# Layer 0's masks through PSUM, fewer small instructions for lists and norms, and a re-ordered layer 3 in a four-layer graph-attention kernel

## The chip, the cores and the metric

The kernel runs on one core of a Trainium2 chip. The core has five instruction queues: PE (the matrix engine; PEld is its weight load, which runs beside the matmuls), DVE (VectorE), ACT (ScalarE), POOL (GpSimd) and SP (SyncE, which here only issues DMAs). Each queue works in order. PE reads from SBUF and writes to PSUM, which has 8 banks of 128 x 512 fp32. The metric is the device time of one execution in microseconds (us), less is better. The kernel before takes 2305.02 us, the median of 3 runs (2301.89 to 2305.65).

## What is computed

There are 4096 nodes with 256 features, and an adjacency matrix of 0.4% ones plus the diagonal. Four layers of graph attention follow each other, each as `x = layernorm(x + gnn(x, adj))`. Layers 0 and 1 have four heads of 64 columns, layer 2 has two heads of 128. Cut to what matters, a head is

```
h   = x @ W                                    # values
e   = leaky_relu(s1[i] + s2[j], 0.2)           # s1, s2: h times two vectors
att = softmax over j of (e where adj[i, j], else -inf)
out = att @ h
```

Layer 3 has one score, but two softmaxes of it, one over `e` and one over `-e`; the second is subtracted, the two results go through one matrix product and an ELU.

## The kernel before

**Tiles and lists.** Rows (destinations) are worked in 32 tiles of 128. Few nodes have an edge into a given tile, so for each tile the kernel makes a list of those that do, in 13 groups of 128, and the compact mask that belongs to it. A 14th group, at place FRONT = 6, is the tile's own 128 nodes, which need no list. So a tile has 14 places, worked in two halves of 7. The lists are made once, while layer 0 runs (`lists`): ACT turns the int32 adjacency into bytes (L373), DVE finds which nodes occur (L377), and per tile `pack` builds 31 one-hot matrices on DVE (L430), with which PE compacts the mask (L436). Each mask row carries four more columns, three of which are the node's number in base 16, so that the matmul compacts the numbers too. ACT copies the 128 mask columns (L443) and, apart, the digit columns (L444) out of PSUM; DVE makes indices of the digits (L448 to L451). The mask goes to DRAM as `maskC`. Ten tiles are packed before layer 0 begins; the other 22 one by one in its first 22 tiles.

**A tile in a layer.** `RowTile.load` issues the DMAs of a half: on SP the score row `S` (L620) and the compact mask `mk` (L622), the tile's own nodes directly (L627), the residual (L926); on POOL one indirect DMA per listed group (L630), 13 per tile, 1456 in all, which gather value rows and scores of 128 nodes into a slot `G`. The slots are a ring; in layer 0 there are 16 of two groups each, some 2.3 tiles. `RowTile.half` computes the weights. exp(leaky_relu) is written as a maximum of an exponential and a constant: for three heads in layers 0 and 1 (both in layer 2) ACT does the exponential for each group (L671), and DVE in one instruction of 896 columns the maximum with LEAST and the product with the mask (L672). The fourth head in layers 0 and 1 needs no exponential: DVE multiplies each group's scores and takes the maximum (L667, seven per half), then multiplies by the mask (L668). In layer 1, and only there, DVE first copies a whole tile's mask bytes as int32 into a PSUM bank (L646), and L668 and L672 read them there; in the other layers they read `mk` in SBUF. Layer 3 has its own form (L658 to L662). PE multiplies weights and values (L680, L683). `finish` divides, adds the residual and calls `norm`, which works out 1/sqrt with 15 small DVE instructions (L945 to L955) for a group of rows' tiles and then scales them (L957); in layer 0 groups are of four up to tile 24, elsewhere of one. The finished tile is projected for the next layer (`Projection`, L532 to L584: transpose, copy, multiply, row, edge), and its row stored to DRAM (L574), where the next layer's gathers read it. The gathers of places 0 to 5 read only nodes of the first 17 tiles (MIX), the others may read any node.

**All-node units.** In layer 2 the last 12 tiles, in layer 3 the last 4, are not listed: blocks of four tiles go over all 32 source tiles (`whole_rows`; L901, L902, L904 to L909, PE L912). A source tile is one unit; `Layer.whole` hands out units between the steps of the listed tiles. In layer 3 a block makes two passes of 32 units; after the first, `positive` copies the four accumulators out of PSUM (L968 on DVE, L971 on ACT), and the second pass uses the same four banks. After the last unit the four tiles are finished together.

**Order.** A step is half a tile: `half_alone` (layers 0 and 1) and `half_with_whole` (layers 2 and 3) trace, one after another, a projection's parts, the half, `finish` of the tile before (in the second step of a tile) and the units. A scheduler then orders each queue.

**PSUM.** Four banks serve accumulators and back-transposes (`ptwo`). The other four are two pools of two (`pair`): by turns all four for the lists and for units (`pfour`), in layer 1 two of them for masks and two for projections.

Of the kernel before, what the change touches and what calls it, by code (L numbers as in the profile page):

```python
# [50 lines left out]
P = 128  # L51
# [23 lines left out]
GROUPED = 24  # L75
# [4 lines left out]
MC = P + 4  # L80
EDGE = 64.0
# [53 lines left out]
def kernel(ctx: ExitStack, tc: tile.TileContext, ins: dict, out: bass.AP):  # L135
# [7 lines left out]
        "idx": const.tile([P, NT, NG], I32, name="idx"),  # L143
# [5 lines left out]
        "maskC": dram.tile([NT, P, NP, P], U8, name="maskC"),  # L149
# [37 lines left out]
class Program:  # L187


    def __init__(self, tc, ctx, ins, out, shared):  # L190
# [10 lines left out]
        self.pair = [self.pool(f"pair{k}", 2, space=PSUM) for k in range(2)]  # L201
        self.pfour = Turns(self.pair)
# [82 lines left out]
    def lists(self, ctx):  # L285
# [15 lines left out]

        node = cst.tile([P, NT], I32, name="node")
# [3 lines left out]
        for k, sh in enumerate((8, 4, 0)):  # L306
            d = cst.tile([P, NT], I32, name=f"d{k}")
            nc.vector.tensor_scalar(d, node, sh, 15, op0=ALU.logical_shift_right, op1=ALU.bitwise_and)
            nc.vector.tensor_copy(dig[:, :, k], d, saturate=False)
# [30 lines left out]
        for j in range(NT):  # L340
            m = 0
            while m < NT:
# [9 lines left out]
                m = e  # L352
        total = cst.tile([P, NT], F32, name="total")
# [3 lines left out]
        class Block:  # L357
# [24 lines left out]
            def places(self):  # L382
# [7 lines left out]
                pt = prog.bank(prog.pfour)  # L390
# [3 lines left out]
                pq = prog.bank(prog.pfour)  # L394
# [19 lines left out]
                self.num = wk.tile([P, BT, NG, 4], F32, name="num")  # L414

            def pack(self, it):
                m, mk = self.blk * BT + it, self.mk
                cm = cmp_.tile([P, NP, P], U8, name="cm")
                nc.scalar.copy(cm[:, FRONT, :], mk[:, m, it, :P])
# [7 lines left out]
                for j in order:  # L427
# [4 lines left out]
                    for k in range(a, a + n):  # L432
                        b, s = divmod(k, 3)
                        if b not in accs:
                            accs[b] = prog.bank(prog.pfour)
# [3 lines left out]
                        if touches[b][-1] == (j, k):  # L439
                            e = min(3, NG - 3 * b)  # L440
                            got = accs[b][:, :e * MC].rearrange("p (s c) -> p s c", c=MC)
                            o = 3 * b + (3 * b >= FRONT)
                            nc.scalar.activation(cm[:, o:o + e, :], got[:, :, :P], AF.Copy, scale=EDGE / 2.0)  # L443
                            nc.scalar.copy(self.num[:, it, 3 * b:3 * b + e, :], got[:, :, P:])  # L444
                nc.sync.dma_start(out=shared["maskC"][m], in_=cm)
                num = self.num[:, it]
                t = wk.tile([P, NG], F32, name="t")
                nc.vector.scalar_tensor_tensor(t, num[:, :, 0], 16.0, num[:, :, 1], op0=ALU.mult, op1=ALU.add)  # L448
                nc.vector.scalar_tensor_tensor(t, t, 16.0, num[:, :, 2], op0=ALU.mult, op1=ALU.add)
                nc.vector.tensor_scalar(shared["idx"][:, m, :FRONT], t[:, :FRONT], float(MIX * P - 1), None, op0=ALU.min)  # L450
                nc.vector.tensor_scalar(shared["idx"][:, m, FRONT:], t[:, FRONT:], float(N - 1), None, op0=ALU.min)  # L451
# [19 lines left out]
        pf = self.bank(self.pfour)  # L471
# [122 lines left out]
class RowTile:  # L594
# [20 lines left out]
    def load(self, half):  # L615
        L, m, n = self.layer, self.m, self.layer.n
        prog, nc, sh = L.prog, L.nc, L.shared
        if half == 0:
            self.S = prog.ld.tile([P, H4, P], F32, name="S")
            nc.sync.dma_start(out=self.S[:, :TERMS[n]], in_=sh["e"][n][m].partition_broadcast(P))  # L620
            self.mk = prog.ld.tile([P, NP, P], U8, name="mk")
# [3 lines left out]
        for pos in range(HALF * half, HALF * (half + 1)):  # L625
            if pos == FRONT:
# [5 lines left out]
                in_offset=bass.IndirectOffsetOnAxis(ap=sh["idx"][:, m, t:t + 1], axis=0))  # L632

    def half(self, half):
# [8 lines left out]
        if n == 1 and half == 0:  # L643

            bank = prog.bank(prog.pair[0])
            nc.vector.tensor_scalar(bank.bitcast(I32)[:, :NP * P // 4],  # L646
                                    self.mk.rearrange("p t i -> p (t i)").bitcast(I32), 0, None,
                                    op0=ALU.bitwise_or)
            self.mk = bank.bitcast(U8)[:, :NP * P].rearrange("p (t i) -> p t i", t=NP)
        mh = self.mk[:, half * HALF:(half + 1) * HALF, :]  # L650
# [13 lines left out]
        else:  # L664
            for h in range(A, T):
                for k in range(HALF):
                    nc.vector.tensor_scalar(w[h][:, k, :], S[:, h, :], d(k, h), LEAST, op0=ALU.mult, op1=ALU.max)  # L667
                nc.vector.tensor_tensor(w[h], w[h], mh, op=ALU.mult)  # L668
# [32 lines left out]
    def finish(self):  # L701
        z = self.layer.positive(self.accs[0]) if self.layer.n == 3 else None
# [3 lines left out]
class Layer:  # L706
# [3 lines left out]
    def __init__(self, prog, n):  # L710
# [7 lines left out]
        self.nxt = self.middle = self.stored = None  # L718
        self.group = []
        self.ready = []  # L720
        self.step = 0

# [11 lines left out]
    def set_banks(self):  # L734
        self.prog.banks = self.prog.ptwo[1] if self.n in (0, 2) else self.prog.pair[1]

    def whole(self, step):

        while self.used < self.total and self.used < self.total * (step + 1) / (2 * self.count - 6):
# [20 lines left out]
    def half_alone(self, m, part):  # L760
# [4 lines left out]
        second = self.n == 0 and m > NT - LEAD and len(self.ready) > 1  # L765
        if self.ready and self.ready[0][0] < self.step and (part == 0 or second):
            self.set_banks()
            if part == 1:
                self.prog.banks = self.prog.pfour
# [22 lines left out]
    def half_with_whole(self, m, part):  # L792
# [8 lines left out]
        if part == 1 or self.tile(m).accs is None:  # L801
            self.tile(m).half(part)
# [6 lines left out]
        if part == 1 and m >= 1:  # L809
# [57 lines left out]
    def whole_rows(self):  # L867
# [3 lines left out]
        for blk in range(NB - WHOLE[n], NB):  # L871
# [5 lines left out]
            for heads in groups:  # L877
# [15 lines left out]
                for j in range(NT):  # L893
# [3 lines left out]
                    for h in heads:  # L897
# [13 lines left out]
                        for it in range(BT):  # L911
                            nc.tensor.matmul(accs[it][:, c:c + Wd], p[:, it, :], v[:, c:c + Wd],  # L912
                                             start=(j == 0 and h == heads[0]), stop=(j == NT - 1),
                                             skip_group_check=True)
                    yield
                if n == 3 and heads[0] == 0:
                    for it in range(BT):
                        zs[it] = self.positive(accs[it], whole=True)
            for it, m in enumerate(tiles):
                self.finish(m, accs[it], self.load_x(m), zs[it])  # L920

# [7 lines left out]
    def norm(self, y, m):  # L929
# [9 lines left out]
        if self.n == 0 and m < GROUPED and len(self.group) < BT:  # L939
# [24 lines left out]
    def positive(self, acc, whole=False):  # L964
# [3 lines left out]
        nc.vector.reciprocal(rec, acc[:, D:Wd])  # L968
        pool = self.prog.bk if whole else self.prog.ep
        z = pool.tile([P, F], F32, name="zw", bufs=BT) if whole else pool.tile([P, F], F32, name="z")  # L970
        nc.scalar.activation(z, acc[:, :D], AF.Copy, scale=rec)  # L971
        return z
# [486 lines left out]
```

## Time and profile before

One profiled execution took 2293.77 us, its span is 2292.0 us; that is 11.25 us (0.5%) under the median of the three timed runs.

| engine | busy us | share of the span | instructions |
|---|---|---|---|
| PE | 2029.3 | 89% | 15689 |
| DVE | 1832.3 | 80% | 6100 |
| ACT | 1752.1 | 76% | 5137 |
| POOL | 1597.3 | 70% | 1596 |

| stretch, us | what runs |
|---|---|
| 0 to 100 | weights, first projections, first lists; the first gather of layer 0 starts at 104 |
| 104 to 637 | layer 0, with the lists beside it; the last one-hot (L430) is at 637 |
| 637 to 811 | the rest of layer 0's gathers; the last one ends at 811 |
| 811 to 1339 | layer 1's gathers; the first that may read any node starts at 857 |
| 1339 to 1707 | layer 2's gathers; units of 12 tiles beside them |
| 1763 to 2261 | layer 3's gathers; units of 4 tiles beside them |
| 2261 to 2292 | the last halves and finishes |

Busy shares are averages over stages with different limits, so each stage is read by itself. An instruction's duration in the profile overlaps the next one's start on DVE and ACT; what it costs a full engine is the distance from its start to that of the instruction that follows it directly. Such distances below are called "start to start", and are medians over the pairs in the timeline.

### The profile page before, as it was taken

To read this page: it belongs to the slowest core of one execution; us is meant where nothing else is said; L and a number is where in the kernel's file an instruction comes from. 1 tells how busy PE (TensorE), PEld (TensorE's weight loads), DVE (VectorE), ACT (ScalarE), POOL (GpSimd) and SP (SyncE) were. 2 spreads that over 40 slices of the span, in tenths; PEclk is the share of its full clock that TensorE was granted. 3 is DMA by queue.
4 is the path that set the end of the run, shared out by engine and by line. 5 is a ranking of instruction groups with operands and counts; after the bars stand their busy time and mean duration, and the time that the engine had idled before them with its cause. 6 is when DMAs were issued, how large, how long until landed. Compare 5 with 4: busy or idle time off the path is not lost. (4 is left out here: it accounts for less than half of the span.)

```text
span 2292.0 us, 49763 instructions
## 1 busy us (share of the span) xinstructions
PE 2029.3 (89%) x15689; PEld 1847.6 (81%) x15689; DVE 1832.3 (80%) x6100; ACT 1752.1 (76%) x5137; POOL 1597.3 (70%) x1596
## 2 busy tenths in 40 slices
PE   4888998998998867999999898989998799979996
PEld 2667887888888767999888887989997688768885
DVE  2999999999987868999888886988976366655567
ACT  4779898997887758998888877988883667666663
POOL 2117887777787777777777777777761677777773
PEclk8989999999999988999999999999999899989998
DMA  8789788775455565666666556777764788888884
GB/s 279 257 259 337 228 265 272 258 262 179 136 154 157 151 203 163 189 187 170 179 167 184 168 153 186 221 203 235 230 199 140 249 263 266 267 252 273 264 251 133
DMA packets 250324, 492.00 MB, mean 215 GB/s; under 512 B 44385, under 2 KB 156610, under 8 KB 249666
## 3 DMA queue, kind: packets, MB, share of 16 engines
q0 software_dynamic: 81536, 245.30, 37.1%
q1 hardware_dynamic: 168514, 243.42, 32.8%
q8 instruction: 126, 2.06, 0.4%
q14 instruction: 148, 1.21, 0.2%
HBM read 436.24 MB, written 52.31 MB: 213 GB/s over the span
## 5 line engine op out<-in xcount | busy, mean ns | idle before, releaser
L630 POOL DMA_INDIRECT G<-vals,idx x1456 | 1584.3, 1088 | 654.1 <-issue 184.3
L671 ACT ACTIVATE w<-S,G 128x128 f32<-128x128 f32 x3248 | 994.0, 391 | 135.0 <-DMA G<-vals,idx 121.4
L680 PE MATMUL bank<-w,G 128*65 128x128 f32 x7168 | 845.5, 279 | 94.7 <-DVE w L668 71.7
L680 PEld LDWEIGHTS bank<-w,G 128*65 128x65 f32 x7168 | 809.4, 142 | 108.6 <-DVE w L668 87.7
L683 PE MATMUL bank<-G,w 128*128 128x257 f32 (+1 forms) x2688 | 496.8, 343 | 32.9 <-DVE w L672 10.4
L683 PEld LDWEIGHTS bank<-G,w 128*128 128x128 f32 x2688 | 437.4, 195 | 83.0 <-ACT z L971 11.6
L672 DVE SCALAR_TENSOR_TENSOR w<-w,mk 128x896 f32<-128x896 f32 x272 | 293.2, 1083 | 36.0 <-ACT w L671 33.9
L912 PE MATMUL bank<-vw,pw 128*128 128x129 f32 (+1 forms) x2048 | 302.2, 304 | 15.8 <-ACT zw L971 14.5
L912 PEld LDWEIGHTS bank<-vw,pw 128*128 128x128 f32 x2048 | 276.4, 193 | 33.0 <-ACT zw L971 14.9
L667 DVE TENSOR_SCALAR w<-S,G 128x128 f32<-128x128 f32 x896 | 238.3, 300 | 76.2 <-DMA G<-vals,idx 74.7
L658 ACT ACTIVATE w<-S,G 128x128 f32<-128x128 f32 x392 | 141.4, 391 | 138.0 <-DMA G<-vals 70.1
L430 DVE TENSOR_SCALAR oh<-iota,place 128x256 bf16<-128x256 f16 (+2 forms) x992 | 222.4, 301 | 8.5 <-PE bank L436 8.4
L672 DVE SCALAR_TENSOR_TENSOR w<-w,bank 128x896 f32<-128x896 f32 x192 | 206.3, 1081 | 8.8 <-ACT w L671 8.7
L436 PE MATMUL bank<-mk,oh 128*128 128x132 fp8e4 x2336 | 187.0, 225 | 14.9 <-DVE oh L430 10.5
L546 PE MATMUL bank<-wext,xT 128*128 128x268 f32 (+3 forms) x640 | 177.3, 408 | 21.6 <-ACT xT L537 18.1
L436 PEld LDWEIGHTS <-oh 128*128 128x128 bf16 x2336 | 143.1, 98 | 54.3 <-DVE oh L430 23.6
L909 DVE TENSOR_TENSOR pw<-pw,mw 128x512 f32<-128x512 f32 x64 | 44.0, 690 | 133.2 <-ACT pw L908 71.9
L546 PEld LDWEIGHTS bank<-wext,xT 128*128 128x128 f32 x640 | 116.6, 199 | 40.0 <-ACT xT L537 20.1
L373 ACT ACTIVATE mk<-raw 128x1024 uint8<-128x1024 int32 x128 | 131.7, 1063 | 17.2 <-DMA raw<-in_adjB_dram 16.7
L901 ACT ACTIVATE pw<-Sw,d 128x512 f32<-128x512 f32 x192 | 132.1, 714 | 14.8 <-PE bank L912 9.5
L902 DVE SCALAR_TENSOR_TENSOR pw<-pw,mw 128x512 f32<-128x512 f32 x192 | 127.6, 689 | 11.9 <-ACT pw L901 11.3
L443 ACT ACTIVATE cm<-bank 128x384 uint8<-128x384 f32 (+1 forms) x160 | 70.2, 450 | 56.4 <-PE bank L436 54.6
(131 smaller groups left out, 1716.3 us busy)
## 6 DMA issues: line engine op xcount, KB each, us to landing
raw<-in_adjB_dram SPq DMA_DIRECT2D x128, 512.0 KB
mk<-maskC SPq DMA_DIRECT2D x112, 224.0 KB
G<-vals,idx POOLq DMA_INDIRECT x1456
S<-edge SPq DMA_DIRECT2D x64, 256.0 KB
vw<-vals SPq DMA_DIRECT2D x96, 129.0 KB
xp<-y SPq DMA_DIRECT2D x96, 128.0 KB
y<-xp SPq DMA_DIRECT2D x96, 128.0 KB
mw<-maskW SPq DMA_DIRECT2D x20, 528.0 KB
```

The costliest lines, as they stand in the source:

```text
L430: nc.vector.tensor_scalar(oh[:, :n * P], iota[:, :n * P], self.place[:, it, j:j + 1], None, op0=ALU.is_equal)
L436: nc.tensor.matmul(accs[b][:, s * MC:(s + 1) * MC], oh[:, (k - a) * P:(k - a + 1) * P], mk[:, j, it, :].bitcast(FP8), start=touches[b][0] ...
L546: nc.tensor.matmul(pp[:, :c1 - c0], self.xT[:, k, :], wext[:, k, c0:c1], start=(k == 0), stop=(k == KT - 1 and brow is None))
L630: nc.gpsimd.indirect_dma_start(out=self.place(pos), out_offset=None, in_=sh["v"][n][:NODES[t], :], in_offset=bass.IndirectOffsetOnAxis(ap= ...
L658: nc.scalar.activation(w[0][:, k, :], S[:, 0, :], AF.Relu, bias=d(k, 0))
L667: nc.vector.tensor_scalar(w[h][:, k, :], S[:, h, :], d(k, h), LEAST, op0=ALU.mult, op1=ALU.max)
L671: nc.scalar.activation(w[h][:, k, :], S[:, h, :], AF.Exp, bias=d(k, h))
L672: nc.vector.scalar_tensor_tensor(w[h], w[h], LEAST, mh, op0=ALU.max, op1=ALU.mult)
L680: nc.tensor.matmul(accs[0][:Wd, h * P:(h + 1) * P], v, w[h][:, k, :], **how)
L683: nc.tensor.matmul(a, w[h][:, k, :], v, **how)
L901: nc.scalar.activation(p, S[:, h], AF.Exp, bias=d)
L912: nc.tensor.matmul(accs[it][:, c:c + Wd], p[:, it, :], v[:, c:c + Wd], start=(j == 0 and h == heads[0]), stop=(j == NT - 1), skip_group_ch ...
```

## The change

Parts:

1. Masks. In layers 0 and 1 each half copies its own half of the mask (7 groups x 132 bytes, 231 words per partition) into half of one PSUM bank, which is kept for both layers; the copy of a whole tile in layer 1 is dropped. `maskC` and `mk` have 132 columns instead of 128.
2. PSUM pools. `two` has two banks, `one` and `last` one each. `last` holds the masks during layers 0 and 1. Lists and layer 1's projections turn over three banks (`pthree`), units still over four.
3. Lists. The digits are scaled so that the copy of the mask (L443) carries them along as bytes; the 160 small ACT copies (L444) go, and four small DVE instructions per tile become three.
4. The fourth head. Two neighbouring groups that share a slot are multiplied by one tensor-tensor instruction of 256 columns with broadcast operands, and the maximum moves to the product with the mask: per half three pairs and one single instead of seven singles.
5. Norms in groups: two in layer 1 up to tile 28 and in most of layer 2, four for layer 3's last four tiles.
6. Layer 3. The copies between the two passes are traced in a step directly after the half, ahead of that step's units, and the next half is queued behind them on DVE and ACT. `finish` of the tile before moves from a tile's second step to its first. The last four tiles are finished one in a step.
7. Layer 1 may project a second row in a tile's second step near its end.

```diff
+GROUPS = (((24, 4),), ((28, 2),), ((16, 2), (20, 1), (31, 2)), ((28, 1), (31, 4)))
...
-        "maskC": dram.tile([NT, P, NP, P], U8, name="maskC"),
+        "maskC": dram.tile([NT, P, NP, MC], U8, name="maskC"),
...
-        self.pair = [self.pool(f"pair{k}", 2, space=PSUM) for k in range(2)]
-        self.pfour = Turns(self.pair)
+        two, one, last = (self.pool(f"pair{k}", 2 - (k > 0), space=PSUM) for k in range(3))
+        self.pfour, self.pthree, self.pmask = Turns((two, one, two, last)), Turns((two, one, two)), last
+        self.masks = None
...
-                            nc.scalar.activation(cm[:, o:o + e, :], got[:, :, :P], AF.Copy, scale=EDGE / 2.0)
-                            nc.scalar.copy(self.num[:, it, 3 * b:3 * b + e, :], got[:, :, P:])
+                            nc.scalar.activation(cm[:, o:o + e, :], got, AF.Copy, scale=EDGE / 2.0)
...
-                nc.vector.tensor_scalar(shared["idx"][:, m, :FRONT], t[:, :FRONT], float(MIX * P - 1), None, op0=ALU.min)
-                nc.vector.tensor_scalar(shared["idx"][:, m, FRONT:], t[:, FRONT:], float(N - 1), None, op0=ALU.min)
+                nc.vector.tensor_tensor(shared["idx"][:, m, :], t, limit, op=ALU.min)
...
-        if n == 1 and half == 0:
-
-            bank = prog.bank(prog.pair[0])
-            nc.vector.tensor_scalar(bank.bitcast(I32)[:, :NP * P // 4],
-                                    self.mk.rearrange("p t i -> p (t i)").bitcast(I32), 0, None,
+        mh = self.mk[:, half * HALF:(half + 1) * HALF, :]
+        if n < 2:
+
+            if prog.masks is None:
+                prog.masks = prog.bank(prog.pmask)
+            there = prog.masks[:, half * BANK // 2:half * BANK // 2 + HALF * MC // 4].bitcast(I32)
+            nc.vector.tensor_scalar(there, mh.rearrange("p t i -> p (t i)").bitcast(I32), 0, None,
                                     op0=ALU.bitwise_or)
-            self.mk = bank.bitcast(U8)[:, :NP * P].rearrange("p (t i) -> p t i", t=NP)
-        mh = self.mk[:, half * HALF:(half + 1) * HALF, :]
+            mh = there.bitcast(U8).rearrange("p (t i) -> p t i", t=HALF)
+        mh = mh[:, :, :P]
...
-                for k in range(HALF):
-                    nc.vector.tensor_scalar(w[h][:, k, :], S[:, h, :], d(k, h), LEAST, op0=ALU.mult, op1=ALU.max)
-                nc.vector.tensor_tensor(w[h], w[h], mh, op=ALU.mult)
+                k = 0
+                while k < HALF:
+                    pos = half * HALF + k
+                    e = 2 if pos % 2 == 0 and k + 1 < HALF else 1
+                    if e == 2:
+                        dd = self.slots[pos // 2][:, :2 * ROW[n]].rearrange("p (t c) -> p t c", t=2)
+                        nc.vector.tensor_tensor(
+                            w[h][:, k:k + 2, :], S[:, h:h + 1, :].to_broadcast([P, 2, P]),
+                            dd[:, :, V + T + h:V + T + h + 1].to_broadcast([P, 2, P]), op=ALU.mult)
+                    else:
+                        nc.vector.tensor_scalar(w[h][:, k, :], S[:, h, :], d(k, h), None, op0=ALU.mult)
+                    k += e
+                nc.vector.scalar_tensor_tensor(w[h], w[h], LEAST, mh, op0=ALU.max, op1=ALU.mult)
...
-        while self.used < self.total and self.used < self.total * (step + 1) / (2 * self.count - 6):
+        while self.between is None and self.used < self.total \
+                and self.used < self.total * (step + 1) / (2 * self.count - 6):
...
-        second = self.n == 0 and m > NT - LEAD and len(self.ready) > 1
+        second = m > NT - (LEAD if self.n == 0 else 6) and len(self.ready) > 1
...
-        if part == 1 or self.tile(m).accs is None:
-            self.tile(m).half(part)
+        with ExitStack() as order:
+            for ins in self.last:
+                order.enter_context(self.prog.tc.issue_after(ins))
+            self.last = ()
+            if part == 1 or self.tile(m).accs is None:
+                self.tile(m).half(part)
+        if self.between is not None:
+
+            self.last = self.between()
+            self.between = None
...
-        if part == 1 and m >= 1:
+        if part == (0 if self.n == 3 else 1) and m >= 1:
             self.tile(m - 1).finish()
...
+                    if n == 3 and heads[0] == 0 and j == NT - 1:
+                        def between(accs=accs):
+                            for it in range(BT):
+                                zs[it], last = self.positive(accs[it], whole=True)
+                            return last
+                        self.between = between
                     yield
...
                 self.finish(m, accs[it], self.load_x(m), zs[it])
+                if n == 3:
+                    yield
...
-        if self.n == 0 and m < GROUPED and len(self.group) < BT:
+        if len(self.group) < next((size for end, size in GROUPS[self.n] if m < end), 1):
             return
```

## The prediction

> **What bounds the kernel now.** I read the slices first, then busy time by stage, then the gathers' groups in two stages, then the timeline around stretched gathers, and last the chain that ended last. The stages (PE, PEld, DVE, ACT, POOL busy; clock; DMA share; GB/s):
>
> ```profile
> 100.00:640.00 540.00, 482.48 (x4805) 431.40 (x4805) 522.37 (x1833) 464.25 (x1474) 383.91 (x304) 0.97 0.76 245
> 640.00:811.00 171.00, 146.63 (x1209) 141.33 (x1207) 137.75 (x396) 134.31 (x462) 136.57 (x114) 0.94 0.54 156
> 857.00:1339.00 482.00, 443.55 (x3736) 417.67 (x3737) 436.97 (x1402) 414.95 (x1392) 365.39 (x383) 0.97 0.63 176
> 1400.00:1700.00 300.00, 288.56 (x2379) 280.84 (x2379) 259.62 (x810) 260.98 (x701) 236.24 (x209) 0.99 0.75 219
> 1796.00:2261.00 465.00, 427.90 (x1923) 369.51 (x1922) 274.34 (x850) 304.58 (x642) 355.89 (x344) 0.96 0.83 260
> ```
>
> While lists are made, DVE is full (522 of 540). In layer 2 PE is (289 of 300). In the other three no engine looks full, but POOL is: every gather is followed by 0.30 us put down to "issue", and the shortest takes 0.946. So POOL's floor is 1.246 us a gather. After the lists the pace is 171/114 = 1.500, in layer 1 482/383 = 1.258, in layer 3 465/344 = 1.352. Why 1.500 and 1.258 differ (gathers from 250 to 600, then from 800 to 1250; then three moments):
>
> ```profile
> L630 POOL DMA_INDIRECT G<-vals,idx x217 | 274.2, 1264 | 77.5 <-issue 27.1 <-ACT w L671 11.8 <-PE bank L680 10.2
> L630 POOL DMA_INDIRECT G<-vals,idx x354 | 341.5, 965 | 110.3 <-issue 46.0 <-PE bank L680 28.0 <-DMA G<-vals,idx 6.7
> ...
> 806.18 1.08 DVE L672 SCALAR_TENSOR_TENSOR w<-w,mk 128x896 f32<-128x896 f32 x1
> 806.26 1.83 POOL L630 DMA_INDIRECT G<-vals,idx  x1 [0.30 <-DVE y L986]
> ...
> 643.63 4.07 POOL L630 DMA_INDIRECT G<-vals,idx  x1 [0.30 <-DVE w L667]
> 643.79 1.09 DVE L672 SCALAR_TENSOR_TENSOR w<-w,mk 128x896 f32<-128x896 f32 x1
> 644.79 1.09 DVE L668 TENSOR_TENSOR w<-w,mk 128x896 f32<-128x896 f32 x1
> 645.79 1.09 DVE L672 SCALAR_TENSOR_TENSOR w<-w,mk 128x896 f32<-128x896 f32 x1
> ...
> 1072.35 0.42 DVE L986 TENSOR_TENSOR y<-y,z 128x256 f32<-128x256 f32 x1
> 1072.44 1.15 POOL L630 DMA_INDIRECT G<-vals,idx  x1 [0.30 <-DVE w L667]
> 1072.68 1.08 DVE L672 SCALAR_TENSOR_TENSOR w<-w,bank 128x896 f32<-128x896 f32 x1
> ```
>
> A gather that starts under an L672 or L668 with both inputs in SBUF stands until that one ends, then needs some 0.8 us more; at 643.63 it stood through three. The third moment shows a 256-column instruction with two SBUF inputs cost 0.2 us, and the L672 that reads a bank cost nothing. So a DVE instruction of length t that holds POOL costs, at one request every 1.25 us, t x t / 2.5 on average. Eight of 1.0 us a tile (start to start) make 3.2 us, 0.246 a gather; measured 1.500 - 1.258 = 0.242.
>
> The end of the span, by the chain:
>
> ```profile
> 2234.97 0.44 DVE y L957
> 2235.43 0.34 SPq L959
> 2235.94 5.77 DMA G<-vals
> 2256.10 23.38 PE bank L683 x98
> ```
>
> A direct load stood on SP behind an output store that waited for a norm; then 23 us of PE work was left in one piece.
>
> **Listing (104 to 637).** DVE bounds, so its start-to-start times add. Per tile, 14 L667 at 0.195 (2.73 us) become 6 pairs, priced by 256-column tensor-tensors at 0.333, and 2 singles: 2.39, so -0.34 (start to start, as all these). Two mask copies are new; L646 takes 0.530 for 448 words, 128x128 operations 0.195, so 231 words about 0.304: +0.61. One index instruction less is -0.05, eight products reading PSUM -0.03 (0.9975 against 1.001 each). Sum +0.19, times 22 tiles +4. Ends: pairs at their profiled 0.42 instead, +0.52 more a tile, +15; relieved gathers (DVE waited 4.6 us on them), -5. The 160 ACT copies (L444, 0.049) and norm work are not what DVE waits for: nothing. Three banks for lists: I followed each accumulator's start to the evacuation that would free its bank; the median slack is 4.5 us, the shortest 0.3: nothing, bounded by 160 starts each 0.5 late at +0 to +5 for the few percent that are near.
>
> **Layer 0 after the lists.** 114 gathers at 1.500. With masks in PSUM eight holds go; six pairs a tile come, 0.333 x 0.333 / 2.5 = 0.044 each, 0.27, and where two or three stand directly together more: I take 0.35 a tile, 0.027 a gather. 114 x (1.500 - 1.258 - 0.027) = -25. PE is next: in this stretch it worked 146.6 us on 9.7 tiles (1086 of 112 matmuls a tile), which would just fill the 146 us left; I give 3 back: **-22**. Ends: -28 (pairs free, PE catches up in the 46 us hand-over to layer 1, which stays) and -15 (three pairs as one hold of 1.0 us: 0.8 a tile, -7; PE gives back 5 more).
>
> **Layer 1.** 383 gathers are 29.5 tiles, POOL-bound at 16.4 us a tile (PE 443.55/29.5 = 15.0, DVE 14.8). Its mask is in PSUM already, so here only the pairs come: 29.5 x 0.35 = **+10**. The lower end is -4: all the stretch over 0.946 that layer 1 shows (402 gathers) is 4.0 us, so the seven L667 that go cannot have cost more. Upper end +24: 0.8 a tile, three pairs in one hold. The copy split in two (0.61 for 0.53) and norms by two lie on DVE, which has 1.6 us a tile to spare: nothing; with that cover gone 29.5 x 0.08 = 2. A row held for its group's partner is stored one tile (16 us) later, hidden as gathers at the front of layer 2 read early rows; the last four tiles are single.
>
> The Trainium skill, "SBUF — State Buffer", section "Who interferes with whom", says that a DVE instruction with two SBUF inputs, but also a scalar one in a two-port mode, shuts GpSimd out while it runs; "VectorE: DVE Perf Modes", section "The perf-mode tier table (the rule you actually need)", lets fp32 scalar operations in SBUF enter such a mode. By that, L667 would hold POOL too (14 x 0.195 x 0.195 / 2.5 = 0.21 a tile), the exchange would be +2 instead of +10, and the sum about 8 lower. The layer 1 gathers at 965 with L667 among them speak against most of it; the row decides.
>
> **Layer 2.** PE-bound, its matmuls unchanged: **0**, between -3 and +3 (norm groups; DVE has 40 of 300 us free).
>
> **Layer 2 to 3.** POOL stood 55.4 us at 1707 until the last row it needs at the front was stored. Stores follow each other some 5 us apart (tile 31 at 1754.0, 16 at 1758.2); listed tiles grouped by two and the last projection standing behind layer 3's first half move two of them. I take **-3**, ends -5 and +5 (one store each way).
>
> **Layer 3.** The pace is 17.6 us a tile against PE's 16.6. PE stands 14.52 us at 2011 for the copies between the passes, and POOL lost 4.0 us there. Copies in a step without units, ahead of the next half's DVE and ACT work, let PE run that half's matmuls: **-4**, bounded by POOL's 4.0 if it is the bound, -10 if the PE stall counts, and +6 if the half queued behind copies (8 instructions, four zw of 0.47 and four reciprocals of 0.17, 2.6 us) and its one step fewer of units is late. `finish` a step earlier issues the output store earlier, so SP's direct load stands behind it less.
>
> **Tail.** Four finishes lay together from 2245.97 to 2255.65 on DVE, ahead of the last half's PE work, which waited 7 us; spread over four steps about half goes: **-3**, ends -6 and 0.
>
> Sum: +4 -22 +10 0 -3 -4 -3 = **-18**: 2293.8 becomes 2275.8 in the profile. The median lies 11.25 above the profiled time; carried over, 2287.
>
> **Rivals.**
> - *Pairs hold POOL longer (the other side).* In `half` the mask copy, three pairs, and a single stand together on DVE. If a gather stands through all (0.30 + 3 x 0.333 = 1.3 us: 0.68 a half, 1.35 a tile, 0.104 a gather), 497 gathers cost 52. All else sums to -31, so it ends at +21, 2326. It decides from 0.062 a gather: layer 1's mean gather 1.02 instead of 0.957. For it: 643.63 stood through three. Against: L986 beside gathers leaves a mean of 979; layer 1's pairs often wait for separate gathers (L667 idle 35 us for them) and so do not stand together. Three pairs as one hold: 0, 2305.
> - *The early finish in layer 3 stalls.* DVE and ACT reach it before PE has ended the tile's matmuls, and the next half is queued behind. Slack is 1.0 us a tile; at 2 us lost over 28 tiles +28, so +17: 2322. Against: DVE is 59% busy there.
> - *Three banks stall the lists.* 0.5 us of evacuation at each of 5 x 22 accumulators: +55, 2342; the slack of 0.3 or more speaks against.
> - *The hand-over eats the gain.* The gathers speed up but PE and the last tile's path do not, so half of the tail's gain returns: about -7, 2298.
>
> **How the numbers follow.** A measurement of this kernel can tell about 0.2% (4.6 us) from no change. The forecast (2287, own range 2270 to 2298) has 0.60; half eaten 0.12, ending faster; pairs 0.14, of which 0.05 same and 0.09 slower; early finish 0.07, 0.02 same and 0.05 slower; banks 0.03; more gain than the ends allow together 0.04. Of the forecast's own, 0.03 is same. Faster 0.73, same 0.10, slower 0.17. For 8 in 10 the range goes from 2260 (low ends of tail, layer 1 and layer 3) to 2310.
>
> **What the new profile would show.** Right: L672 in layer 0 reads a bank; gathers after the lists have a mean under 1.0 us (pace 1.28) instead of 1.26; layer 1's mean is 0.98; the listing period is 21.7 us; the 14.5 us PE stall is gone; PE's last piece is shorter. Wrong, if layer 1's mean is over 1.02, if L436 waits for L443, if in layer 3 the reciprocal of `positive` waits for PE and the pace passes 17.6 a tile, or if the hand-over from layer 0 to 1 grows beyond 46 us.

## The result, and the profile after

The changed kernel takes 2286.9 us, the median of 4 executions (2283.55 to 2292.53); the kernel before, beside it, 2303.45 us. The ratio is 0.9932, with a 95% interval from 0.9907 to 0.9957. A second comparison, told below, gave 0.9941 (0.9924 to 0.9958). The forecast was 2287, faster; the total and its direction hold. The parts do not: the listing stage was missed by 20 us, and two other stages by 7 and 8.5 us the other way.

The table gives the length of each stage in us. "Lists" ends with the last one-hot, "rest of layer 0" with layer 1's first gather, "layer 1" and "layer 2" run from first gather to first gather, with layer 2's cut at its 20th tile; "stall" is from there to layer 3's third tile, "layer 3" runs to the start of its last gather, "end" from there. Each of the two kernels has two profiles.

| stage | before | before, second | after | after, second | change of the means | forecast |
|---|---|---|---|---|---|---|
| lists | 637.6 | 640.8 | 663.2 | 664.2 | +24.5 | +4 |
| rest of layer 0 | 173.4 | 173.8 | 144.6 | 144.7 | -29.0 | -22 |
| layer 1 | 528.0 | 527.6 | 530.3 | 528.4 | +1.5 | +10 |
| layer 2 | 349.9 | 348.0 | 348.2 | 351.5 | +0.9 | 0 |
| stall | 114.7 | 115.7 | 117.0 | 115.4 | +1.0 | -3 |
| layer 3 | 456.8 | 455.5 | 453.0 | 451.0 | -4.2 | -4 |
| end | 31.7 | 32.2 | 30.1 | 29.8 | -2.0 | -3 |
| span | 2292.0 | 2293.7 | 2286.4 | 2284.8 | -7.3 | -18 |

The spans of the profiled executions differ by 7.3 us, the timed medians by 16.6 in the first comparison and 12.7 in the second. Both profiled executions of the kernel before (2293.8 and 2295.5 us) lie under the medians timed beside them (2303.5 and 2296.7), and 17 executions of it spread from 2285 to 2309. What differs between them was not seen in a profile, so 5 to 9 us of the measured gain have no place in the table.

Where the time went is seen best in the windows of the two layer-0 stages (PE, PEld, DVE, ACT, POOL busy; clock; DMA share; GB/s). Before, cut at the end of its lists:

```profile
100.00:637.00 537.00, 479.48 (x4775) 428.61 (x4774) 519.37 (x1827) 462.64 (x1467) 381.21 (x303) 0.97 0.76 245
637.00:811.00 174.00, 149.63 (x1240) 144.12 (x1237) 140.75 (x402) 135.92 (x470) 139.27 (x115) 0.94 0.54 156
```

Its gathers in the second of these windows (count, busy us and mean ns, idle time before them):

```profile
L630 POOL DMA_INDIRECT G<-vals,idx x115 | 140.7, 1224 | 35.0 <-issue 16.5 <-PE bank L680 7.3 <-DMA G<-vals,idx 3.7
```

After, cut in the same way, windows and gathers:

```profile
100.00:663.00 563.00, 490.98 (x4777) 435.36 (x4776) 522.73 (x1711) 455.69 (x1326) 305.01 (x307) 0.96 0.74 235
663.00:808.00 145.00, 140.77 (x1247) 136.68 (x1245) 139.69 (x371) 134.41 (x471) 106.10 (x111) 1.00 0.68 194
L634 POOL DMA_INDIRECT G<-vals,idx x111 | 107.3, 967 | 39.2 <-issue 14.6 <-PE bank L696 7.9 <-ACT w L687 6.0
```

The same PE work (some 4775 and 1245 matmuls) takes 26 us more while lists are made and 29 less afterwards. In the first stage DVE's busy time hardly grew (519 to 523 us), but it is no longer full: 563 - 523 = 40 us free, against 18. POOL is busy 76 us less there, and the stage is no shorter for it. In the second stage POOL's relief arrives in full, and PE (141 of 145) and DVE (140) are now as full as POOL (106 us busy, and some 0.30 us more before each of 111 gathers).

The gathers' groups of after (250 to 600, then 860 to 1330) and their surroundings in the timeline:

```profile
L634 POOL DMA_INDIRECT G<-vals,idx x200 | 201.4, 1007 | 151.2 <-PE bank L696 69.7 <-issue 37.0 <-PE bank L442 12.1
L634 POOL DMA_INDIRECT G<-vals,idx x369 | 358.4, 971 | 112.5 <-issue 50.6 <-PE bank L696 30.2 <-DMA G<-vals,idx 7.6
...
705.24 1.09 DVE L684 SCALAR_TENSOR_TENSOR w<-w,bank 128x896 f32<-128x896 f32 x1
705.42 0.95 POOL L634 DMA_INDIRECT G<-vals,idx  x1 [0.31 <-DVE w L678]
706.24 1.08 DVE L688 SCALAR_TENSOR_TENSOR w<-w,bank 128x896 f32<-128x896 f32 x1
706.67 0.95 POOL L634 DMA_INDIRECT G<-vals,idx  x1 [0.30 <-PE bank L696]
```

In layer 0, gathers that took 1264 ns on average now take 1007; beside a product that reads a bank a gather runs its plain 0.95 us. But the idle time in front of 200 of them is 151 us where it was 78 for 217: POOL now waits for slots of the ring, which PE frees (L696, 70 us of it).

At the pass boundary of layer 3, PE's longest wait from 1796 to the end before, and then all its waits there after (us in total, times, longest):

```profile
PE bank L912 <- ACT zw L971: 14.5, 1, 14.5
...
PE bank L699 <- DVE w L666: 11.8, 6, 6.8
PE bank L699 <- ACT z L1002: 10.7, 8, 2.7
PE bank L938 <- ACT zw L1002: 2.9, 1, 2.9
```

The single stall of 14.5 us for the copies (13.9 in the second profile of before) is 2.9 (1.9).

### The profile page after: what moved, and what is told of

It reads as the page before. It is cut to its first block, busy times and chain, and to the rows that moved or that the text cites. A ratio compares the mean times of both kernels' runs of the same rounds, so it can differ in the third digit from the quotient of the medians.

```text
span 2286.4 us, 49074 instructions
## 1 busy us (share of the span) xinstructions
PE 2026.1 (89%) x15689; PEld 1835.8 (80%) x15689; DVE 1798.3 (79%) x5317; ACT 1741.5 (76%) x4977; POOL 1493.2 (65%) x1596
## 4 chain that ended last, share of the span: by engine, by line
PE 51%; DVE 15%; DMA 14%; ACT 11%; issue 5%; POOL 3%; SPq 0%; DVEq 0%; ACTq 0%; POOLq 0%
PE bank L699 16%; PE bank L696 14%; PE bank L938 10%; DMA G<-vals,idx 8%; ACT w L687 6%; PE bank L550 5%; PE bank L442 4%; POOL G L634 3%; DVE w L688 3%; DMA raw<-in_adjB_dram 2%; DVE w L684 2%; DVE oh L436 2%; DVE w L678 1%; DMA G<-vals 1%; ACT mk L380 1%
## 5 line engine op out<-in xcount | busy, mean ns | idle before, releaser
L634 POOL DMA_INDIRECT G<-vals,idx x1456 | 1480.2, 1017 | 754.2 <-issue 205.0
L696 PE MATMUL bank<-w,G 128*65 128x128 f32 x7168 | 842.9, 277 | 102.0 <-DVE w L684 79.0
L696 PEld LDWEIGHTS bank<-w,G 128*65 128x65 f32 x7168 | 800.6, 140 | 120.8 <-DVE w L684 91.3
L699 PE MATMUL bank<-G,w 128*128 128x257 f32 (+1 forms) x2688 | 491.3, 340 | 33.6 <-DVE w L666 11.8
L699 PEld LDWEIGHTS bank<-G,w 128*128 128x128 f32 x2688 | 431.8, 193 | 83.5 <-DVE w L666 14.7
L688 DVE SCALAR_TENSOR_TENSOR w<-w,bank 128x896 f32<-128x896 f32 x384 | 411.7, 1081 | 21.0 <-ACT w L687 20.5
L678 DVE TENSOR_TENSOR w<-S,G 128x256 f32<-128x256 f32 x384 | 154.4, 418 | 51.8 <-DMA G<-vals,idx 48.9
L927 ACT ACTIVATE pw<-Sw,d 128x512 f32<-128x512 f32 x192 | 131.6, 714 | 17.0 <-PE bank L938 12.7
L684 DVE SCALAR_TENSOR_TENSOR w<-w,bank 128x896 f32<-128x896 f32 x128 | 138.7, 1083 | 0.9
L688 DVE SCALAR_TENSOR_TENSOR w<-w,mk 128x896 f32<-128x896 f32 x80 | 86.7, 1087 | 43.1 <-ACT w L687 42.0
## 6 DMA issues: line engine op xcount, KB each, us to landing
mw<-maskW SPq DMA_DIRECT2D x20, 528.0 KB
```

The costliest lines, as they stand in the source:

```text
L634: nc.gpsimd.indirect_dma_start(out=self.place(pos), out_offset=None, in_=sh["v"][n][:NODES[t], :], in_offset=bass.IndirectOffsetOnAxis(ap= ...
L678: nc.vector.tensor_tensor(w[h][:, k:k + 2, :], S[:, h:h + 1, :].to_broadcast([P, 2, P]), dd[:, :, V + T + h:V + T + h + 1].to_broadcast([P ...
L684: nc.vector.scalar_tensor_tensor(w[h], w[h], LEAST, mh, op0=ALU.max, op1=ALU.mult)
L688: nc.vector.scalar_tensor_tensor(w[h], w[h], LEAST, mh, op0=ALU.max, op1=ALU.mult)
L696: nc.tensor.matmul(accs[0][:Wd, h * P:(h + 1) * P], v, w[h][:, k, :], **how)
L699: nc.tensor.matmul(a, w[h][:, k, :], v, **how)
```

## The experiments

Two sets of four kernels were run on two chips where the kernel before takes 2296.7 and 2296.6 us. A third set fell on a chip with another behaviour and is told at the end. Diffs are against the changed kernel unless it says otherwise.

**The kernel before, a second profile.** No edit.

> The kernel before, unchanged, for a second profile. In the first two profiles the lists end at 641 (before) and 667 us (after): the listing stage looks 22 us longer where the forecast gave +4, while the timed medians differ by 17 in the other direction and the profile of before lay 10 us under its median. If the stage times are typical, lists end again between 636 and 646 and tile 22's first gather starts near 612; if the first profile had a lucky listing stage, lists end at 650 or later, the gathers after them again take 1.50 us each (locks theory), and the listing stage of the changed kernel is only some 10 us longer.

2295.48 us. Lists end at 640.8, the gathers after them have a mean of 1240 ns. The first profile was typical by stage, so the 24.5 us by which the listing stage grew are real, and the forecast's +4 is wrong.

**More buffers for the packed mask rows.** In after, ACT's first copy for a tile stands behind the store of the rows three tiles back; before it did so less. ACT's waits from 220 to 640, before and then after (us in total, times, longest):

```profile
ACT cm L419 <- DMA maskC<-cm: 7.3, 2, 4.1
```

```profile
ACT cm L425 <- DMA maskC<-cm: 21.0, 4, 6.1
```

```diff
-        wk, cmp_ = pool("iwk", 2), pool("cm", 3)
+        wk, cmp_ = pool("iwk", 2), pool("cm", 4)
```

> The changed kernel with four buffers instead of three for the packed mask rows. Theory 'list buffers': the listing stage grew because ACT's first copy of a tile (L425) stands for the store of the mask rows three tiles back (21.0 us in four stalls of 6, against 7.3 us before); then these waits fall under 4 us, lists end near 652 instead of 667, and the time falls by about 13 to 2274. Rival 'DVE work': the added mask copies and slower pairs are what lengthens the stage; then lists still end near 665 and the time stays within 4 of 2287. Rival 'three banks': the same as DVE work here.

2284.93 us, ratio 0.9943 (0.9919 to 0.9967): the same as the changed kernel. Lists end at 657.2, 6 us earlier, but ACT still stands 22.4 us before this copy over layer 0, against 23.6. With four buffers the copy stands earlier in ACT's queue, again directly behind the store that frees its buffer. So a fourth buffer does not remove the waits, and lists do not end near 652 as that theory had it; what the waits themselves cost is not told by this run.

**Layer 0's masks back in SBUF.**

```diff
-        if n < 2:
+        if n == 1:
             if prog.masks is None:
```

> The changed kernel, layer 0's products reading the mask in SBUF as before (no mask copy in layer 0; everything else kept, the copy by halves in layer 1 too). Locks theory: the gathers after the lists go from a mean near 0.97 back to 1.20 or more, that stretch grows by 25 us or more; the listing stage loses 44 copies of 0.30 (13 us) if DVE is full there; sum 2287 + 25 - 13 = 2299. Rival 'the place of the mask does not matter, the fewer small instructions gave the gain': gathers stay near 0.97 and the time falls by the copies, to 2274.

2288.79 us, ratio 0.9963 (0.9947 to 0.998), between the two expectations. Its two layer-0 windows, and its gathers in the second:

```profile
100.00:636.00 536.00, 482.71 (x4776) 433.42 (x4774) 510.83 (x1666) 456.35 (x1328) 376.36 (x305) 0.96 0.77 246
636.00:806.00 170.00, 144.63 (x1200) 137.36 (x1199) 133.57 (x333) 132.93 (x459) 135.10 (x112) 0.95 0.55 155
L634 POOL DMA_INDIRECT G<-vals,idx x112 | 135.9, 1214 | 35.2 <-issue 16.5 <-PE bank L696 4.9 <-DMA G<-vals,idx 2.7
```

The gathers after the lists are stretched again (mean 1214 ns), that stage is 170 us, as the locks theory has it (products with two SBUF inputs hold POOL). But lists end at 636, 27 us earlier than with masks in PSUM, twice what the forecast's price for the copies gives. Gain and loss nearly cancel: layer 0 ends at 806.3 here and at 807.8 and 808.9 in the changed kernel. This kernel's lists use three banks, have the pairs and carry the digits with the mask; so none of these lengthens the listing stage by itself.

**The copy made, but not read.** In layer 0 the products read the mask in SBUF, and the copy's result isn't used there.

```diff
-            mh = there.bitcast(U8).rearrange("p (t i) -> p t i", t=HALF)
+            if n == 1:
+                mh = there.bitcast(U8).rearrange("p (t i) -> p t i", t=HALF)
```

> The changed kernel, layer 0 still copying each half's mask into PSUM, but its products reading the mask in SBUF (the copy's result is not used in layer 0). It tells the copy's own price in the listing stage from that of the read. If DVE's time for the copies lengthens the stage: lists end near 663, as with the copy used, and gathers are stretched as well (mean 1.2), so the time is 20 to 27 above the changed kernel's, near 2310. If it is the products reading a bank (or gathers running freely) that lengthens the stage, lists end near 640 and the time is near 2290.

2303.01 us, ratio 1.0026 (1.0008 to 1.0044). Lists end at 648.8, the rest of layer 0 takes 175 us. Its listing window:

```profile
100.00:649.00 549.00, 490.51 (x4786) 437.66 (x4787) 523.01 (x1711) 458.51 (x1335) 374.93 (x304) 0.96 0.75 241
```

Neither expectation is met alone: the copies themselves cost 648.8 - 636.2 = 12.6 us, near the 44 x 0.304 = 13.4 of the forecast's price, and they are DVE's work (busy 511 with masks in SBUF, 523 here; idle 25 and 26). The other 15 us, up to 663 or 664, come only when the products read the bank, and add nothing to DVE's busy time (523), only idle time (40). From 230 to 620 it goes from 10.8 to 23 us (it was 11.3 with masks in SBUF), and ACT's standing before its first copy of a tile, over layer 0, from 8.2 to 23.6 (12.0 with masks in SBUF). The queues of the two kernels are ordered differently as well, so whether the freely running gathers or the order makes these waits is not told apart.

**Late masks.** Tiles of layer 0 that run while lists are made read SBUF; from tile 22 on they copy into PSUM.

```diff
-        if n < 2:
+        if n == 1 or n == 0 and self.m >= NT - LEAD:
             if prog.masks is None:
```

> The changed kernel itself, timed beside the next ones and profiled a second time. If its listing stage is typical, lists end near 663 us again (637 and 641 in two profiles of the kernel before), DVE idles 20 us or more between 230 and 620, and the ratio to the kernel before is 0.991 to 0.996.

> The changed kernel, but in layer 0 only tiles 22 and later, which run after the last list is made, copy their masks into PSUM; tiles 0 to 21 read them in SBUF. Theory 'PSUM masks pay only where POOL is the bound': the lists end near 637 as in the two kernels with SBUF masks, the gathers after them have a mean near 0.97 and a pace near 1.32, so layer 0's gathers end near 637 + 113 x 1.30 = 784 instead of 806, and the time is 22 below the changed kernel's, near 2264. Rival 'the listing stage grew through something else (three banks, digit copies, pairs)': lists end at 655 or later and the gain is under 8. Rival 'handed back': the lists and gathers end early, but layer 1's first all-node gather waits for the last projections, and under 10 of the 22 arrive at layer 1.

The changed kernel, again: 2283.98 us, ratio 0.9941, lists end at 664.2, DVE idle 23.6. With late masks: 2262.94 us, ratio 0.9851 (0.9829 to 0.9873). Its windows:

```profile
100.00:637.00 537.00, 482.53 (x4777) 429.45 (x4775) 511.21 (x1669) 456.34 (x1328) 388.23 (x303) 0.97 0.76 245
637.00:783.00 146.00, 139.75 (x1227) 134.43 (x1226) 137.53 (x359) 133.31 (x465) 111.27 (x115) 1.00 0.67 189
```

The first stage is that of the kernel before, the second that of the changed one. Layer 0 ends at 782.6, 26 us earlier, and all of it goes through: layer 1's gathers begin and end some 26 us earlier, the span is 26.5 us shorter, the timed median 21 (expected: 22). Together with masks in SBUF, whose kernel differs only in the ten tiles after the lists (2288.79, ratio 0.9963), this shows both halves apart: masks in PSUM gain 24 us in layer 0 where POOL is the bound, after the lists, and lose 26 beside the lists, where DVE had hardly any time to spare.

**Pairs and singles.** With all of layer 0 in PSUM, and then with late masks, the pairs are undone:

```diff
-                k = 0
-                while k < HALF:
-                    pos = half * HALF + k
...
-                    k += e
+                for k in range(HALF):
+                    nc.vector.tensor_scalar(w[h][:, k, :], S[:, h, :], d(k, h), None, op0=ALU.mult)
```

> The changed kernel with the fourth head multiplied by seven single tensor-scalar instructions a half instead of three pairs and one single (the maximum stays in the product with the mask). Locks theory with the price measured in the profile: layer 1's gathers fall from a mean near 0.970 to 0.957 (5 us in 416), the listing stage takes 0.34 a tile more (+7), the stretch after the lists gains 1 to 3: 2287, unchanged within 4. By the forecast's price (10 us in layer 1, 3 after the lists) 2281. Rival 'pairs hold POOL no more than singles do' (both lock): layer 1's mean does not move and the time is +7, 2294.

> The same with the fourth head's multiplications as seven singles a half instead of three pairs and one single. From the earlier run with singles: layer 1's gathers 0.955 instead of 0.971, 7 us, and 4 us after the lists. If that adds up, 2254 and 8 to 11 below the kernel with late masks and pairs; if singles save only where the masks were all in PSUM, equal to it within 4.

Singles: 2276.92 us, ratio 0.9916 (0.9893 to 0.9939), against 0.9941 with pairs, and lower than any of its expectations (2281 at best). Late masks with singles: 2260.48 us, ratio 0.9843 (0.9826 to 0.9859), the fastest kernel run, 23.5 us below the changed one and 36 below the one before; it beats late masks with pairs by less than its interval, not by the 8 to 11 us hoped for. Layer 1's gathers (860 to 1330) with singles, to be set beside the 971 ns of after:

```profile
L634 POOL DMA_INDIRECT G<-vals,idx x374 | 357.2, 955 | 113.9 <-issue 49.4 <-PE bank L686 31.4 <-DMA G<-vals,idx 9.8
```

So the pairs cost layer 1's gathers 16 ns each, 6 us in 383. Over the whole layer the four profiles with singles have means of 953 to 959 ns, the six with pairs 965 to 974. Layer 1 takes 523.8 and 523.3 us with singles, 528 to 532 in the kernels with pairs of these two sets. In the listing stage the price has the other sign, if DVE is full: with late masks lists end at 643.7 with singles and 637.2 with pairs (forecast: 22 x 0.34 = 7.5), which takes back what layer 1 gained. Where DVE idles there anyway, in the changed kernel, nothing is seen (662.9 and 663.2). The stall between layers 2 and 3 was 7 us shorter in the first kernel with singles, and not in the second (109.5 and 116.6), so it can't be put down to the singles; those 7 us are most of what the first kernel gained beyond its expectation.

**The third set.** These four ran on a chip where the kernel before takes 2807.89 us and PE stands for long stretches with no cause in view, so they answer little of what they were meant to.

```diff
# layer 3 as before
-        if self.between is not None:
-            self.last = self.between()
-            self.between = None
...
-        if part == (0 if self.n == 3 else 1) and m >= 1:
+        if part == 1 and m >= 1:
...
-                    if n == 3 and heads[0] == 0 and j == NT - 1:
...
+                if n == 3 and heads[0] == 0:
+                    for it in range(BT):
+                        zs[it], _ = self.positive(accs[it], whole=True)
...
-                if n == 3:
-                    yield
# groups as before
+GROUPS = (((24, 4),), (), (), ())
# late masks alone, against the kernel before
-        if n == 1 and half == 0:
+        if half == 0 and (n == 1 or n == 0 and self.m >= NT - LEAD):
# late masks (that edit is not shown again), pairs only in layer 0's tiles 0 to 21
-                    e = 2 if pos % 2 == 0 and k + 1 < HALF else 1
+                    e = 2 if n == 0 and self.m < NT - LEAD and pos % 2 == 0 and k + 1 < HALF else 1
```

> The changed kernel with layer 3 traced as before: the copies between the two passes directly after the last unit of the first pass, finish of the tile before in a tile's second step, the last four tiles finished together. The forecast gave these parts 4 and 3 us. By the profiles the gathers of layer 3 (third tile to last) take 452 us instead of 456 and the end after the last gather 30 instead of 32. If these are the parts' doing: PE's stall of 14.5 us at the pass boundary is back (2.9 in the changed kernel), gathers 456, end 32, the time near 2290. If the gain came from elsewhere (norm groups, free DVE), both stage times and the time stay: 2284 within 3.

> The changed kernel with norms grouped as before (by four in layer 0, one by one in layers 1 to 3). The forecast put this at nothing: DVE has 1.6 us a tile to spare in layer 1 and 40 of 300 us in layer 2, so the time stays within 3 of 2284 and the gathers of layers 1 and 2 take as long as in the changed kernel (487 and 348 us). If the small instructions did count, layer 2 or the stall between layers 2 and 3 (57 us) is longer by 3 us or more; if holding a row for its partner costs, that stall is shorter.

> The kernel before with one edit: in layer 0, tiles 22 and later copy their whole mask into a bank as layer 1 does. It tells what the masks alone are worth where POOL bounds. Lists end at 638 to 641 as before, the gathers after them take 1.27 instead of 1.53 us, and by the end of layer 0's gathers 29 us are gained; layer 1 keeps its mean of 0.955. So 2297 - 29 = 2268 on this chip. If the rest of the change carries a good part of the 34 us that the late-masks kernel gains, this one stays above 2275.

> The kernel with late masks, with the pairs kept in layer 0's tiles 0 to 21, where DVE is full, and seven singles a half from tile 22 on and in layer 1, where POOL is. If pairs save DVE time and cost POOL time: lists end at 637 (644 with singles there), the pace after them is 1.267, layer 1's gathers have a mean of 0.954, and the time is 6 below the kernel with singles throughout, 2254. If the lists' end does not carry through to the end, 2260.

Layer 3 as before: 2795.11 us, ratio 0.996 (0.9939 to 0.998). Groups as before: 2805.24, 1.0002 (0.9976 to 1.0027). Late masks alone: 2810.14, 1.0013 (0.9989 to 1.0037). Late masks with pairs in the listing stage: 2770.3, 0.9885 (0.985 to 0.992). The changed kernel was not run on this chip, so the first two have nothing to be set against, and what the groups and layer 3's parts are worth by themselves stays open. The 14 us stall at the pass boundary doesn't show there with layer 3 as before, since PE itself is late. The third still shows something. Its waits of PE over the whole span, and its window after the lists:

```profile
PE bank L680 <- issue: 140.7, 170, 2.6
PE bank L436 <- issue: 89.1, 76, 11.5
...
849.00:1028.00 179.00, 146.31 (x1110) 135.82 (x1110) 128.68 (x374) 122.63 (x428) 102.39 (x108) 0.90 0.50 143
```

The gathers are as short as hoped (949 ns), but 108 of them take 179 us, with POOL 57% and PE 82% busy, and the whole kernel is not faster. The likely reading is that PE is the late one here, so that freeing POOL is worth nothing; but the kernel before was not profiled on this chip, and how long its stage is there is not known. That late masks alone give the 29 us on a chip like the first two was not shown; with the rest of the change they give them, as the windows of late masks show.

## Why the prediction was right or wrong

- *POOL bounds after the lists and in layer 1, and products with two SBUF inputs hold it*: right, shown by masks in SBUF (1214 ns) against in PSUM (967). The term was -22 and is -29. The pace was about right: 114 gathers in 171 - 22 = 149 us are 1.31 us each, measured 1.32 (from 1.53, cut at the end of the lists instead of at 640). The rest of the size is that 109 gathers were left when the lists ended instead of 113, some 6 us, which belongs with the longer listing stage. PE filled its stage as the forecast feared (141 of 145 us), and layer 1 did not start later for it.
- *Listing +4*: the step that failed, in its premise that DVE bounds and so its start-to-start times add up to the stage. The sum of the work was good: from 100 us to the last one-hot DVE is busy 520.0 and 522.2 us before, 522.9 and 522.0 after, the copies add 11.8 (511.0 to 522.8; 13.4 in the forecast), and pairs against singles measured 6.5 for 7.5. What it put at nothing was DVE's idle time, which went from 17.6 and 18.6 us to 40.3 and 42.3; that is more than the whole error of 20. ACT stands 23.6 instead of 7.7 us over layer 0 for stored mask rows; that these waits are what DVE waits for was not shown. Relieved gathers, which the forecast had at nothing or at a gain of 5, came with a longer stage. The two ends given for this term (-5 and +15) did not hold it.
- *Layer 1, +10 from the pairs*: the mechanism is right, the size was too large. Layer 1's mean went from 953 and 956 ns to 966 and 970, some +5 us over its gathers; 16 ns a gather was measured against 27 assumed. The addition for pairs that stand together (0.27 to 0.35 a tile) was not needed. The trace shows who holds whom: of layer 1's 416 gathers, the 43 to 46 that had a pair running on DVE 0.1 us after their start took 153 and 179 ns longer than the usual 946 (two profiles of after), and the 57 to 71 that had a single running there 18 to 31 ns (four profiles with singles), 1.0 to 1.8 us in all. The front gathers of layer 1 gained 4 us (46.3 and 47.4 to 43.0 and 42.8 until the first gather of any node, which no longer waits 3 us); this was not in the sum, and leaves +1.5.
- *Layer 1 by the skill's rule.* The Trainium skill, "SBUF — State Buffer", section "Who interferes with whom", says that a scalar DVE instruction in a two-port mode holds GpSimd too. If the singles were such instructions, they would cost 0.21 / 13 = 16 ns a gather, an estimate with that rule. This case's trace speaks against that: all that stretches layer 1's gathers in the kernels with singles, 953 to 959 ns over the usual 946, is less than that. The measured +5 lies between the +2 of that reading and the +10 of the forecast.
- *Layer 2, 0*: right (+0.9, less than its two profiles differ). *Stall, -3*: not seen (+1.0).
- *Layer 3, -4, and the end, -3*: -4.2 and -2.0, in both pairs of profiles. PE's stall fell from 14.5 to 2.9 us as expected, and the gain has the size of the 4 us that POOL lost there. That these parts made it, and not the norm groups, was not shown. One reason given was wrong: SP's wait for the norm of the output store did not shrink (68.6 us in 19 waits before, 83.9 in 20 after). PE's 16.6 us a tile, from which the slack of the early finish was taken, does not come out of the row shown either: 427.90 us on 344 / 13 = 26.5 tiles are 16.2.
- *The rivals.* Pairs hold POOL longer: excluded, the mean would be 1020 and is 971. Three banks stall the lists: excluded by masks in SBUF, whose lists over three banks end at 636. The early finish stalls layer 3: its pace went down. The hand-over eats the gain: excluded, it is 43 us instead of 46, and the 26 us of late masks pass through whole.
- *The total.* By its steps the forecast came out at -18; the stages give -7 (errors of +20 and -7 in layer 0, -8.5 in layer 1, +4 at the stall), and the medians -17 and -13. That 2287 met 2286.9 is partly chance: the forecast for the profile, 2275.8, was missed by 12 us (2288.2), and the 11.25 us carried over from profile to median did not recur, as the median after lies 1.3 us under its profiled execution. The two errors cancel.
- *Two readings.* The gathers' 0.946 us is their usual time (the median), not their shortest, which is 0.940; and 0.30 us is the least there is between two gathers, whatever the profile names as its cause. The floor of 1.246 us a gather holds as the usual pace.

## What to carry to other kernels

An edit that relieves one engine at the price of another is priced stage by stage: the same mask copy saves 24 to 29 us after the lists, where POOL is the bound, and costs about 26 beside them, where DVE had hardly any time to spare, and choosing it by the stage (one condition on the tile's number) took a kernel from 0.994 to 0.985. A term that assumes an engine is full needs a look at whether the change itself lets it wait: the sum of its work is then only a lower bound. And when a total agrees with a forecast, the stages should still be compared one by one.

## What was not expected of the hardware

- A 256-column fp32 product of two SBUF operands delays the stream of gathers by 16 x 13 / 6 = 35 ns on average, a little under t x t / 2.5 = 44 for its 0.333 us; the 896-column one fits that formula (0.242 us a gather measured, 0.246 worked out).
- Fourteen 128-column fp32 multiplications a tile by a value per partition, all in SBUF, stretch a gather that starts under one by only 18 to 31 ns. They take about 1.0 ns a column (0.195 us for 128; 0.323 for 256 in L957, start to start). The one-hots, whose input and output have 16 bits, take 0.26 (0.163 us for 128 columns, 0.229 for 384), and in the listing stage of after and its second profile the 91 gathers with a one-hot running 0.1 us after their start were 67 and 57 ns longer than the usual 946. In the kernel with singles, in the same stretch (230 to 640), it is 91 ns under a one-hot and 37 under a single. One-hots stand in rows, so part of this can be several in turn; but scalar instructions are not alike here in how they hold POOL.
- The stage in which POOL was relieved of 76 us of stretched gathers became longer, not shorter; of the 27 us that masks in PSUM add to it, 12.6 are the copies, and 15 come with the products' reading PSUM, by a way that is not settled.
